# A transformer decoder layer with packed 4-bit weights: float16 weights from dequantization, and sixteen feed-forward chains run four at a time beside attention

## The chip, the cores and the metric

The kernel runs on one core of one Trainium2 chip. The metric is the time of one launch on the device, in microseconds. The engines are TensorE (PE; its weight loads appear as PEld), VectorE (DVE), ScalarE (ACT), GpSimd (POOL) and SyncE (SP), which here issues DMAs. Each engine works through its own queue in order, and waits for the others through semaphores.

## The reference, cut to what matters

Eight sequences (blocks b = 0 to 7) of 128 tokens with 512 features pass through causal self-attention, one cross attention against a context, and a gated feed-forward whose weights are packed 4-bit integers with group scales and zeros (GPTQ). The reference, shortened:

```
x = x + attn(layernorm(x), w_q, w_k, w_v, w_o)       # 32 heads of 128, 8 key/value heads
q = layernorm(x)
x = x + softmax(ctx @ q.T, axis=1) @ ctx             # key and value are both the context
def dequant_gptq(qweight, scales, zeros, groupsize): # groups of 128 rows
    zp = (z + 1.0) * s
    return q * s[g] - zp[g]
x2 = layernorm(x)                                    # 1024 x 512
gate, up = x2 @ Wg, x2 @ Wu                          # 512 -> 1376
x = x + ((gate * sigmoid(gate) * up) @ Wd).astype(float16)   # 1376 -> 512
```

The softmax of the cross attention divides by sqrt(128 context rows). Layernorm has no weights.

## The kernel before, in words

**Precision.** Most matmuls run on float16 pairs. A float32 value is split into a high part (`ah`, `qh`, `hi`) and a low part, the difference (`al`, `ql`, `lo`), and `mm3` (lines 159 to 165) adds three products. `split` (116) makes the high part on ACT and the low part on DVE or POOL. `convert` (349) scales a raw tile and splits it: by default with a POOL multiplication, an ACT copy and a POOL subtraction, and with `direct=True` with one scaled ACT copy (351) and one DVE multiply-subtract (352).

**Attention.** The work goes in 64 steps, one per key/value head group g (0 to 7) and block b. The last sixteen steps are (6, 0..3), (7, 0..3), (6, 4..7), (7, 4..7). A step takes the scores and softmax of a later block (`att_s`, 539), the projections of a later unit (`proj_q` and others), the output projection of the block before (`att_o`, 605, which adds to the residual `xr` on DVE at line 614) and the probabilities times values (`att_v`, 591). Probabilities `pb` are transposed to `pt` by a DMA on SP (588). PSUM has eight banks in four tags of two (186): "j" for projections, "s" for scores, "a", and "o" for outputs.

**Quantized weights.** In steps 8 to 42, 35 chunks are unpacked by `dequant` (738): a shift and mask, and then `q - 1 - z` written as int8 into `n8` (761). Scales aren't applied there: a feed-forward chain is a sum over groups, and between two groups the sum in PSUM is multiplied by the ratio of their scales. Before TensorE can use them, the int8 values are cast to float16: gate tiles on ACT (`nf_load`, 1024), up tiles on DVE (1026) and down tiles on ACT (`down_w`, 1162), each 128x512. From the fourth on, gate and up tiles go into buffers of the query weights (tags `wqh`, `wql`), and so wait until the projections have read these. These casts are called in steps 52 to 62.

**Cross attention.** The context is loaded from step 43 on (`c_load`, 911) and split by `c_prep` (915): POOL multiplies (919), ACT copies, POOL subtracts. A block whose attention has ended at step `done` gets `xA` (LayerNorm `norm_T` and a DMA transpose to `qT`, 907) one step later, `xB` (scores, softmax) two steps later, and `xC` (product, addition to `xr`) with `h3_load` (LayerNorm, transpose to `h3`, 1030) three steps later. Work due after step 63 goes into the event list below.

**Feed-forward.** Tokens are taken in two halves of 512. A half has 22 gate and up chains of four rounds (`gate_up`, 1130) and four down chains of eleven (`down`, 1164). A round (`Chain.emit`, 1107) is two matmuls (1114, 1115) into a bank, and then a rescaling of that bank, in turns on ACT (1123) and DVE (1125). A gate chain ends with Silu on ACT (1140); an up chain ends with a DVE product (1145), a high part (1151) and a low part (1152). Silu and the exponential need different tables on ACT, so a change between them issues a table load.

**What sets the order.** `events` holds the rounds with a slot number each (1203 to 1223). Four slots go with each of the last four steps (60 to 63), between the parts of attention; what is left follows after the last step. Chains 0 to 6 start two slots apart, and so run two at a time in the "j" banks (`EARLY = 7`); later ones start a slot apart and take "j", "s" and "o" in turn. Down chains start at slot `D0` = 29, the second half at `G1` = 40, its down chains at `D1` = 62. The order that is written is given to a scheduler, which places each engine's instructions by priority with its own model of time. `in_order` fixes the order on PE until step 59 and on POOL until the end of attention.

**Memory.** Pools are stacked from two sides. `xa` (right) holds context and cross-attention tiles; `fw` and `fp` (left, from step 52) hold float16 weights and products; high and low products `it` lie in query buffers (`qp`).

Of the kernel before, what the change touches and what calls it, by code (L numbers as in the profile page):

```python
# [8 lines left out]
F32 = mybir.dt.float32  # L9
# [1 line left out]
F16 = mybir.dt.float16  # L11
BF16 = mybir.dt.bfloat16
I32 = mybir.dt.int32
I8 = mybir.dt.int8
AF = mybir.ActivationFunctionType
ALU = mybir.AluOpType
PSUM = bass.MemoryType.PSUM
# [31 lines left out]
XPSCALE = 2.0**15  # L49
ROOT = 2.0**-104  # L50

NF0 = 3


@with_exitstack
def tile_decoder(
# [21 lines left out]
    def pool(name, bufs=1, **kw):  # L78
        return tc.alloc_tile_pool(name=name, bufs=bufs, **kw)
# [450 lines left out]
    def run(gen):  # L530
        for _ in gen:
            pass
# [72 lines left out]
    def att_o(g, b):  # L605
# [11 lines left out]


    sF = {}
    n8 = {  # L620
        "g": nqp.tile([P, KT, INTER], I8, name="n8g"),
        "u": nqp.tile([P, KT, INTER], I8, name="n8u"),
        "d": nqp.tile([P, NFT, H], I8, name="n8d"),
    }
    quant = {
        "g": (gq, gz, gs, KT, INTER),
# [111 lines left out]
    def dequant(m, g, c0, c1, after):  # L738
        qsrc = quant[m][0]
        n = c1 - c0  # L740
        rows = min(16, qsrc.shape[0] - g * 16)
        p = rows * 8
        qr = deqp.tile([P, H], I32, name="qr", tag="qr", bufs=2)
        nc.sync.dma_start(
            qr[:p, :n],
            qsrc[g * 16 : g * 16 + rows, c0:c1]
            .rearrange("r n -> r () n")
            .to_broadcast([rows, 8, n]),
        )
        zi = deqp.tile([P, H], I32, name="zi", tag="zi", bufs=2)  # L750
        row = zrow[m] + g
        nc.sync.dma_start(
            zi[:p, :n],
            zt["d"][row : row + 1, c0:c1].to_broadcast([p, n]),
        )
        qi = deqp.tile([P, H], I32, name="qi", tag="qi", bufs=1)
        ins = nc.vector.tensor_scalar(
            qi[:p, :n], qr[:p, :n], sh[:p], 15, ALU.logical_shift_right, ALU.bitwise_and
        )
        issue_after(ins, after)  # L760
        nc.vector.scalar_tensor_tensor(
            n8[m][:p, g, c0:c1], qi[:p, :n], -1.0, zi[:p, :n], ALU.add, ALU.subtract
        )

    chunks = []
# [143 lines left out]
            issue_after(ins, pace["dma"])  # L909

    def c_load(b):
        raw_t["c", b] = c = xa.tile([P, H], F32, name="c", tag="c", bufs=3)
        nc.sync.dma_start(c, cx[b])

    def c_prep(b):
        scales("c", b)
        ctx_scale(b)
        c = raw_t.pop(("c", b))
        ins = nc.gpsimd.tensor_tensor(
            c, c, scx[:, b : b + 1].to_broadcast([P, H]), ALU.mult  # L920
        )
        issue_after(ins, pace["mul"])
        cp = xa.tile([P, 2, H], F16, name="cp", tag="cp", bufs=B)
        split(cp[:, 0, :], cp[:, 1, :], c, nc.gpsimd)
        fl["c", b] = cp

    def norm_T(b, dst):
# [75 lines left out]
    for b in range(B):  # L1003
        at_x(XC + b, lambda b=b: c_load(b))
        at_x(XC + b + 1, lambda b=b: sumsq("c", b, 0, 0))
        at_x(XC + b + 3, lambda b=b: c_prep(b))
        done = steps.index((NG - 1, b))
        tail_x.setdefault((done + 1, 0), []).append(lambda b=b: xA(b))
        tail_x.setdefault((done + 2, 1), []).append(lambda b=b: xB(b))
        tail_x.setdefault((done + 3, 0), []).append(lambda b=b: (xC(b), h3_load(b)))  # L1010

    nf = {}

    def nf_load(m, t):
        w = min(P, INTER - t * P)
        if t < NF0:
            nf[m, t] = fw.tile([P, KT, P], F16, name="nf", tag="nf", bufs=2 * NF0)
        else:
            nf[m, t] = wqp.tile(
                [P, KT, P], F16, name="nf", tag={"g": "wqh", "u": "wql"}[m]  # L1020
            )
        src = n8[m][:, :, t * P : t * P + w]
        if m == "g":
            nc.scalar.copy(nf[m, t][:, :, :w], src)
        else:
            nc.vector.tensor_copy(nf[m, t][:, :, :w], src)

    h3 = {}

# [58 lines left out]

    FFN_MEM = len(steps) - 3 * HB
    FFN0 = len(steps) - HB
    PER_STEP = 4
    EARLY = 7
    ring = ["j", "s", "o"]
    count = [0, 0]

    class Chain:
# [8 lines left out]
        def emit(self, r):  # L1107
            if r == 0:
                count[0] += 1
                tag = "j" if count[0] <= EARLY else ring[count[0] % 3]  # L1110
                self.ps = bank(tag, [P, TH], "ps_c")
            ps = self.ps[: self.w]
            lh, rh, rl = self.parts(r)
            nc.tensor.matmul(ps, lh, rh, start=r == 0, stop=False, skip_group_check=r > 0)  # L1114
            nc.tensor.matmul(ps, lh, rl, start=False, stop=True, skip_group_check=r > 0)  # L1115
            if r == self.rounds - 1:
                self.finish(ps)
                return
            sc = self.ratios()[: self.w, r : r + 1]
            count[1] += 1  # L1120
            act = count[1] % 2 if self.act is None or r < 8 else self.act
            if act:
                nc.scalar.activation(ps, ps, AF.Copy, scale=sc)  # L1123
            else:
                nc.vector.tensor_scalar(ps, ps, sc, None, ALU.mult)  # L1125
# [4 lines left out]
    def gate_up(half, t, m):  # L1130
        w = min(P, INTER - t * P)

        def parts(g):
            return nf[m, t][:, g, :w], h3[half][:, 0, g, :], h3[half][:, 1, g, :]

        def finish(ps):
            sc = sF[m][:w, t, :]
            if m == "g":
                sg = fp.tile([P, TH], F32, name="sg", tag="sg")
                nc.scalar.activation(sg[:w], ps, AF.Silu, scale=sc)  # L1140
                sg_t[half, t] = sg
# [4 lines left out]
            if t < NFT - 1:  # L1146
                it = qp.tile([P, 2, TH], F16, name="it", tag="q" + "hl"[t % 2])
            else:
                it = fw.tile([P, 2, TH], F16, name="it", tag="it", bufs=1)
            eng = nc.vector if half and t >= NFT - 2 else nc.gpsimd  # L1150
            nc.vector.tensor_copy(it[:w, 0, :], pr[:w])  # L1151
            eng.tensor_tensor(it[:w, 1, :], pr[:w], it[:w, 0, :], ALU.subtract)  # L1152
            it_t[half, t] = it

        return Chain(KT, w, lambda: rT[m][:, t, :], parts, finish)

    nd_t = {}

    def down_w(g):
        w = min(P, INTER - g * P)  # L1160
        nd_t[g] = fw.tile([P, H], F16, name="nfd", tag="nfd", bufs=NFT)
        nc.scalar.copy(nd_t[g][:w], n8["d"][:w, g, :])

    def down(half, ct):
        cs = slice(ct * P, (ct + 1) * P)

        def parts(g):
            w = min(P, INTER - g * P)
            it = it_t[half, g]
            return nd_t[g][:w, cs], it[:w, 0, :], it[:w, 1, :]  # L1170

        def finish(ps):
            o = late[0].tile([P, TH], F32, name="oT", tag="oT", bufs=4)
# [21 lines left out]

    late = []

    def free_xa():
        xa.release()
        late.append(pool("late", side="right", reuse_waits="tile"))  # L1200


    NC = 2 * NFT
    events = []
    D0 = NC + EARLY
    G1 = D0 + NFT
    D1 = G1 + NC
    for half, (gs_, ds_) in enumerate([(0, D0), (G1, D1)]):
        for c in range(NC):
            ch = gate_up(half, c // 2, "gu"[c % 2])  # L1210
            st = gs_ + (c if half else c + min(c, EARLY))
            for r in range(KT):
                events.append((st + r, 1, c, lambda ch=ch, r=r: ch.emit(r)))
        for ct in range(KT):
            ch = down(half, ct)
            for r in range(NFT):
                st = ct * (0.5 if half else 1)
                events.append((ds_ + st + r, 1, NC + ct, lambda ch=ch, r=r: ch.emit(r)))
    for i, k in [i for i in tail_x if i[0] >= len(steps)]:
        slot = PER_STEP * (i - FFN0) + 1 + 2 * k  # L1220
        events.append((slot, 0, 1, lambda fs=tail_x.pop((i, k)): [f() for f in fs]))
    events.append((PER_STEP * (len(steps) + 5 - FFN0), 0, 1, free_xa))
    events.sort(key=lambda e: e[:3])

    def traced_after(n, engine, earlier):
# [16 lines left out]
    def tail_step(i):  # L1242
# [14 lines left out]
        for f in tail_x.pop((i, 0), ()):  # L1257
            f()
        run(parts)
        slots(3)  # L1260
        att_v(g, b)
        slots(4)
# [15 lines left out]
    for i in range(len(steps)):  # L1278
        known = len(nc.cur_bb.bb.instructions)
        if i == XC:  # L1280
            deqp.release()
            xa = pool("xa", 2, side="right", reuse_waits="tile")
        if i == FFN_MEM:
            rawp.release()
            fw = pool("fw", reuse_waits="tile")
            fp = pool("fp", 2, reuse_waits="tile")
        if i == FFN0:
            xt.update(s="a", o="a")
        pace["dma"] = pt_dma[steps[i + 1]] if i >= TAIL and steps[i + 1 :] and steps[i + 1] in pt_dma else None
# [17 lines left out]
            inter_scale()  # L1307
        for f in x_steps.pop(i, ()):
            f()
        for t in range(NFT):  # L1310
            if i == (FFN_MEM + 1 + t if t < NF0 else XATT - 4 + t):
                nf_load("g", t)
                nf_load("u", t)
        for g in range(NFT):
            if i == FFN_MEM + g:
                down_w(g)
        if i < 5 * HB:
            traced_after(known, last_h.ins.engine, last_h)
        if i == TAIL - 1:
# [8 lines left out]
    for e in events:  # L1328
        e[3]()

    for pl in (late[0], wvp, wkp, wqp, hp, fp, fw, qp, kp, vp, work, wop, psum, dram, nqp):
        pl.release()
    for pl in (small, xres, const):
        pl.release()
# [50 lines left out]
```

## Time and profile before

| | us |
|---|---|
| median of 3 runs | 676.97 (676.77 to 679.08) |
| the profiled execution | 678.71 |
| its span, first to last instruction | 676.7 |
| 512-column matmul, duration; start to start | 0.38; 0.215 |
| int8 to float16 cast on ACT (L1024, L1162); on DVE (L1026), least to most | 0.61; 0.36 to 2.67 |
| context: POOL multiply (L919), ACT copy, POOL subtract | 1.05, 0.62, 1.16 |
| rescaling on DVE (L1125), on ACT (L1123) | 0.75, 0.66 |
| high part of a product on DVE (L1151), low part on POOL (L1152) | 0.50, 1.15 |
| output addition on DVE (L614) | 0.75 |
| first feed-forward matmul; last attention output; first matmul of the second half | 518.7; 551.7; 601.4 |

A row of a timeline has the start in us from the beginning of the span, the duration, the engine, the line of the kernel, the instruction, `output<-inputs` by the program's names, and shapes; "x4" is four in a row. In brackets stand the idle time before it and the instruction that ended that. A row of the waits has the total, the number, and the longest.

### The profile page before, as it was taken

The page shows a single profiled execution, that of the slowest core. Times are in us where ns is not written, and L with a number is a line of the kernel's source. Part 1 is how long each engine was busy: PE and PEld are TensorE (multiplying, and loading weights), DVE is VectorE, ACT ScalarE, POOL GpSimd, SP SyncE. Part 2 cuts the span into 40 slices and gives each one's busy share as a digit, 9 for nine tenths or more (in the row PEclk, how much of TensorE's full clock was granted, in tenths as well). Part 3 has the DMA queues.
Part 4 walks back from the last instruction along what each step waited for, and adds up shares of the span by engine and source line. Part 5 has one row for each costly group of instructions (what it writes and reads, how often), then busy time and mean ns, then how long its engine had stood idle before and what let it go on. Part 6 is the DMA issues. An engine that isn't in the chain of part 4 may idle for free.

```text
span 676.7 us, 12449 instructions
## 1 busy us (share of the span) xinstructions
PE 639.2 (94%) x3978; PEld 341.6 (50%) x3978; DVE 480.2 (71%) x1504; ACT 453.2 (67%) x1261; POOL 400.6 (59%) x583
## 2 busy tenths in 40 slices
PE   8798999999999999999999999989989988999995
PEld 4365555455555555555555564544545443444442
DVE  6756587765757777676768464676777767988996
ACT  4587486655657574666667666796666667978674
POOL 5658287844747795555588497876775426521310
PEclk9988999999999999999999999999999999999998
DMA  9266344665453756455554525224433232202002
GB/s 309 49 154 176 97 62 117 163 126 148 112 155 87 188 128 157 104 159 127 160 142 109 134 37 136 54 57 87 84 74 56 55 59 48 47 16 62 1 1 62
DMA packets 117757, 69.34 MB, mean 102 GB/s; under 512 B 84174, under 2 KB 100577, under 8 KB 117692
## 3 DMA queue, kind: packets, MB, share of 16 engines
q1 hardware_dynamic: 117692, 68.55, 42.7%
q8 instruction: 31, 0.51, 0.3%
q14 instruction: 34, 0.28, 0.1%
HBM read 42.12 MB, written 2.20 MB: 65 GB/s over the span
## 4 chain that ended last, share of the span: by engine, by line
PE 54%; POOL 14%; DVE 9%; ACT 9%; issue 7%; DMA 6%; SPq 0%; POOLq 0%; DVEq 0%; ACTq 0%
PE ps_o L165 5%; PE ps_c L1114 5%; PE ps_o L163 5%; PE ps_o L164 5%; PE ps_c L1115 5%; PE ps_q L163 5%; PE ps_q L164 5%; PE ps_q L165 4%; DMA pt<-pb 3%; POOL pb L120 3%; POOL s L574 2%; DVE ps_c L1125 2%; POOL wol L120 2%; POOL rawo L357 1%; POOL wql L120 1%
## 5 line engine op out<-in xcount | busy, mean ns | idle before, releaser
L517 ACT ACTIVATE s<-s,negm 128x64 f32<-128x64 f32 (+1 forms) x256 | 93.2, 366 | 35.3 <-DVE negm L560 35.1
L165 PE MATMUL ps_o<-woh,al 128*128 128x512 f16 x256 | 97.3, 380 | 3.4 <-DVE al L120 3.2
L163 PE MATMUL ps_o<-woh,ah 128*128 128x512 f16 x256 | 97.3, 380 | 2.1 <-ACT ah L117 1.9
L163 PE MATMUL ps_q<-hT,wqh 128*128 128x512 f16 x256 | 97.4, 380 | 1.9 <-DVE ql L120 1.0
L165 PE MATMUL ps_q<-hT,wql 128*128 128x512 f16 x256 | 97.3, 380 | 0.0
L164 PE MATMUL ps_o<-wol,ah 128*128 128x512 f16 x256 | 97.3, 380 | 0.0
L164 PE MATMUL ps_q<-hT,wqh 128*128 128x512 f16 x256 | 97.3, 380 | 0.0
L614 DVE SCALAR_TENSOR_TENSOR xr<-ps_o,unsc,xr 128x512 f32<-128x512 f32 x64 | 47.8, 747 | 45.9 <-PE ps_o L165 42.4
L120 POOL TENSOR_TENSOR pb<-s,pb 128x256 f16<-128x256 f32 (+1 forms) x128 | 73.0, 585 | 10.3 <-ACT pb L117 8.6
L560 DVE CUSTOM_DVE_ANT_0 s<-ps_sc,mask,soft 128x64 f32<-128x64 f32 (+1 forms) x256 | 67.2, 310 | 7.3 <-PE ps_sc L165 6.6
L1114 PE MATMUL ps_c<-h,nf 128*128 128x512 f16 (+1 forms) x176 | 66.6, 379 | 3.9 <-ACT sg L1140 1.6
L1115 PE MATMUL ps_c<-h,nf 128*128 128x512 f16 (+1 forms) x176 | 66.6, 379 | 0.0
L574 POOL TENSOR_TENSOR s<-s,rec 128x128 f32<-128x128 f32 (+1 forms) x128 | 62.7, 510 | 4.5
L117 ACT CAST pb<-s 128x128 f16<-128x128 f32 (+1 forms) x128 | 43.2, 350 | 32.3 <-POOL s L574 31.1
L527 POOL TENSOR_SCALAR rec<-rec 128x4 f32<-128x4 f32 x64 | 14.7, 230 | 82.7 <-DVE rec L525 80.5
L120 DVE TENSOR_TENSOR ql<-ps_q,qh 128x512 f16<-128x512 f32 x64 | 43.9, 686 | 25.5 <-ACT qh L117 25.1
L1152 POOL TENSOR_TENSOR it<-pr,it 128x512 f16<-128x512 f32 (+1 forms) x20 | 23.1, 1154 | 63.9 <-DVE it L1151 53.3
L357 POOL TENSOR_TENSOR rawo<-rawo,sco 128x512 f32<-128x512 f32 x30 | 31.1, 1038 | 29.3 <-DVE sco L313 29.3
L120 DVE TENSOR_TENSOR al<-ps_at,ah 128x512 f16<-128x512 f32 x64 | 43.8, 684 | 6.5 <-ACT ah L117 6.3
L517 ACT ACTIVATION_READ_ACCUMULATOR s<-s,negm 128x1 f32 x256 | 48.1, 188 | 0.0
L117 ACT CAST ah<-ps_at 128x512 f16<-128x512 f32 x64 | 37.2, 581 | 14.8 <-PE ps_n L291 7.1
L1123 ACT ACTIVATE ps_c<-ps_c,rTu 128x512 f32<-128x512 f32 (+1 forms) x57 | 36.7, 661 | 12.9 <-PE ps_c L1115 12.3
(219 smaller groups left out, 1733.8 us busy)
## 6 DMA issues: line engine op xcount, KB each, us to landing
rawq<-in_L_attn_w_q_dram SPq DMA_DIRECT2D x8, 1024.0 KB, 6.5
rawo<-in_L_attn_w_o_dram SPq DMA_DIRECT2D x8, 1024.0 KB, 5.4
zi<-zd SPq DMA_DIRECT2D x26, 256.0 KB, 3.7
vd<-v SPq DMA_DIRECT2D x64, 64.0 KB, 2.4
qr<-_L_ffn_down_qweight_dram SPq DMA_DIRECT2D x10, 256.0 KB, 3.3
xr<-in_x_dram SPq DMA_DIRECT2D x8, 256.0 KB, 5.2
rawk<-in_L_attn_w_k_dram SPq DMA_DIRECT2D x8, 256.0 KB, 3.3
rawv<-in_L_attn_w_v_dram SPq DMA_DIRECT2D x4, 512.0 KB, 7.7
```

What stands on the lines that cost most here:

```text
L117: a = nc.scalar.copy(hi, src)
L120: b = (lo_eng or nc.vector).tensor_tensor(lo, src, hi, ALU.subtract)
L163: nc.tensor.matmul(ps, lh, rh, start=start and i == 0, stop=False)
L164: nc.tensor.matmul(ps, lh, rl, start=False, stop=False)
L165: nc.tensor.matmul(ps, ll, rh, start=False, stop=stop and i == n - 1)
L357: a = nc.gpsimd.tensor_tensor(raw, raw, wide.to_broadcast(list(raw.shape)), ALU.mult)
L517: exp = nc.scalar.activation(v, v, AF.Exp, bias=negm[:, j : j + 1], scale=-1.0, accum_out=sums[:, j : j + 1],)
L560: nc.vector.tensor_tensor_reduce(view, flat(ps, cols[j]), masks[j // 2], soft_t[g][:, j % 2 : j % 2 + 1], BIG, ALU.add, ALU.min, negm,)
L574: mul = nc.gpsimd.tensor_tensor(v, v, rec[:, 2 * k : 2 * k + 2].unsqueeze(2).to_broadcast([P, 2, (k + 1) * HQ]), ALU.mult,)
L614: return nc.vector.scalar_tensor_tensor(xr[b], ps, unsc_t[g], xr[b], ALU.mult, ALU.add)
L1114: nc.tensor.matmul(ps, lh, rh, start=r == 0, stop=False, skip_group_check=r > 0)
L1115: nc.tensor.matmul(ps, lh, rl, start=False, stop=True, skip_group_check=r > 0)
```

## The change

1. `dequant` writes float16 (`nf`) in place of int8 (`n8`); `nf_load`, `down_w` and the pool `fw` are gone, and chains read `nf` directly.
2. `c_prep` uses the direct form of `convert`: one scaled ACT copy, one DVE multiply-subtract.
3. `EARLY` is 16. These sixteen chains start one slot apart from slot 2 on, four at a time, in the banks of "j", "o", "j", "s" in turn. The six gate and up chains after them in the first half, and all of the second half, have their rounds 1.25 slots apart. `D0` is 24, so `G1` is 35 and `D1` 57.
4. Products `it` take query-weight buffers for the first eight and last four up chains, and query buffers between. In the second half the high part of the first nine goes to POOL.
5. `xC` and `h3_load` of blocks 0 to 2 come after the projections of their step.
6. The context has a pool of its own (`xc`, right), freed at slot 34 in place of 36; `xa` is opened on the left at step 52.

The diff, cut to its core:

```diff
-    n8 = {
-        "g": nqp.tile([P, KT, INTER], I8, name="n8g"),
...
+    nf = {
+        "g": nqp.tile([P, KT, INTER], F16, name="nfg"),
...
-            n8[m][:p, g, c0:c1], qi[:p, :n], -1.0, zi[:p, :n], ALU.add, ALU.subtract
+            nf[m][:p, g, c0:c1], qi[:p, :n], -1.0, zi[:p, :n], ALU.add, ALU.subtract
...
-        ins = nc.gpsimd.tensor_tensor(
-            c, c, scx[:, b : b + 1].to_broadcast([P, H]), ALU.mult
-        )
-        issue_after(ins, pace["mul"])
-        cp = xa.tile([P, 2, H], F16, name="cp", tag="cp", bufs=B)
-        split(cp[:, 0, :], cp[:, 1, :], c, nc.gpsimd)
+        cp = xc.tile([P, 2, H], F16, name="cp", tag="cp", bufs=B)
+        hi, lo = convert(cp[:, 0, :], cp[:, 1, :], c, scx[:, b : b + 1], True)
+        issue_after(hi, pace["exp"])
...
-        tail_x.setdefault((done + 3, 0), []).append(lambda b=b: (xC(b), h3_load(b)))
+        tail_x.setdefault((done + 3, 2 if b < HB - 1 else 0), []).append(lambda b=b: (xC(b), h3_load(b)))
...
-    EARLY = 7
+    EARLY = 16
...
-                tag = "j" if count[0] <= EARLY else ring[count[0] % 3]
+                tag = "sjoj"[count[0] % 4] if count[0] <= EARLY else ring[count[0] % 3]
...
-            return nf[m, t][:, g, :w], h3[half][:, 0, g, :], h3[half][:, 1, g, :]
+            return nf[m][:, g, t * P : t * P + w], h3[half][:, 0, g, :], h3[half][:, 1, g, :]
...
-            eng = nc.vector if half and t >= NFT - 2 else nc.gpsimd
-            nc.vector.tensor_copy(it[:w, 0, :], pr[:w])
-            eng.tensor_tensor(it[:w, 1, :], pr[:w], it[:w, 0, :], ALU.subtract)
+            hi_eng = nc.gpsimd if half and t < NFT - 2 else nc.vector
+            lo_eng = nc.vector if half and t >= NFT - 2 else nc.gpsimd
+            hi_eng.tensor_copy(it[0][:w], pr[:w])
+            lo_eng.tensor_tensor(it[1][:w], pr[:w], it[0][:w], ALU.subtract)
...
-    D0 = NC + EARLY
+    D0 = NC + 2
...
-            st = gs_ + (c if half else c + min(c, EARLY))
+            st = gs_ + c
             for r in range(KT):
-                events.append((st + r, 1, c, lambda ch=ch, r=r: ch.emit(r)))
+                events.append((st + (r if c < EARLY and not half else r * 1.25), 1, c, lambda ch=ch, r=r: ch.emit(r)))
...
-        for t in range(NFT):
-            if i == (FFN_MEM + 1 + t if t < NF0 else XATT - 4 + t):
-                nf_load("g", t)
-                nf_load("u", t)
-        for g in range(NFT):
-            if i == FFN_MEM + g:
-                down_w(g)
```

More of the change, by code (lines that the diff above doesn't have):

```diff
@@ L13 @@
 I32 = mybir.dt.int32
-I8 = mybir.dt.int8
 AF = mybir.ActivationFunctionType
@@ L50 @@
 ROOT = 2.0**-104
-NF0 = 3
 @with_exitstack
@@ L619, in tile_decoder @@
     sF = {}
-    n8 = {
-        "g": nqp.tile([P, KT, INTER], I8, name="n8g"),
-        "u": nqp.tile([P, KT, INTER], I8, name="n8u"),
-        "d": nqp.tile([P, NFT, H], I8, name="n8d"),
+    nf = {
+        "g": nqp.tile([P, KT, INTER], F16, name="nfg"),
+        "u": nqp.tile([P, KT, INTER], F16, name="nfu"),
+        "d": nqp.tile([P, NFT, H], F16, name="nfd"),
     }
@@ L911, in c_load @@
     def c_load(b):
-        raw_t["c", b] = c = xa.tile([P, H], F32, name="c", tag="c", bufs=3)
+        raw_t["c", b] = c = xc.tile([P, H], F32, name="c", tag="c", bufs=3)
         nc.sync.dma_start(c, cx[b])
@@ L1009, in tile_decoder @@
         tail_x.setdefault((done + 2, 1), []).append(lambda b=b: xB(b))
-        tail_x.setdefault((done + 3, 0), []).append(lambda b=b: (xC(b), h3_load(b)))
[L1012 to L1026, printed above, removed]
+        tail_x.setdefault((done + 3, 2 if b < HB - 1 else 0), []).append(lambda b=b: (xC(b), h3_load(b)))
     h3 = {}
@@ L1145, in finish @@
             nc.vector.scalar_tensor_tensor(pr[:w], ps, sc, sg[:w], ALU.mult, ALU.mult)
-            if t < NFT - 1:
-                it = qp.tile([P, 2, TH], F16, name="it", tag="q" + "hl"[t % 2])
-            else:
-                it = fw.tile([P, 2, TH], F16, name="it", tag="it", bufs=1)
-            eng = nc.vector if half and t >= NFT - 2 else nc.gpsimd
-            nc.vector.tensor_copy(it[:w, 0, :], pr[:w])
-            eng.tensor_tensor(it[:w, 1, :], pr[:w], it[:w, 0, :], ALU.subtract)
+            u = half * NFT + t
+            if 8 <= u < 8 + 10:
+                it = qp.tile([P, 2, TH], F16, name="it", tag="q" + "hl"[u % 2])
+                it = it[:, 0, :], it[:, 1, :]
+            else:
+                it = [
+                    wqp.tile([P, TH], F16, name="it" + p, tag="wq" + p) for p in "hl"
+                ]
+            hi_eng = nc.gpsimd if half and t < NFT - 2 else nc.vector
+            lo_eng = nc.vector if half and t >= NFT - 2 else nc.gpsimd
+            hi_eng.tensor_copy(it[0][:w], pr[:w])
+            lo_eng.tensor_tensor(it[1][:w], pr[:w], it[0][:w], ALU.subtract)
             it_t[half, t] = it
         return Chain(KT, w, lambda: rT[m][:, t, :], parts, finish)
[L1157 to L1162, printed above, removed]
     def down(half, ct):
@@ L1169, in parts @@
             it = it_t[half, g]
-            return nd_t[g][:w, cs], it[:w, 0, :], it[:w, 1, :]
+            return nf["d"][:w, g, cs], it[0][:w], it[1][:w]
         def finish(ps):
@@ L1196, in tile_decoder, with free_xc @@
     late = []
-    def free_xa():
-        xa.release()
+    def free_xc():
+        xc.release()
         late.append(pool("late", side="right", reuse_waits="tile"))
@@ L1204, in tile_decoder @@
     events = []
-    D0 = NC + EARLY
+    D0 = NC + 2
     G1 = D0 + NFT
     D1 = G1 + NC
-    for half, (gs_, ds_) in enumerate([(0, D0), (G1, D1)]):
+    for half, (gs_, ds_) in enumerate([(2, D0), (G1, D1)]):
         for c in range(NC):
             ch = gate_up(half, c // 2, "gu"[c % 2])
-            st = gs_ + (c if half else c + min(c, EARLY))
+            st = gs_ + c
             for r in range(KT):
-                events.append((st + r, 1, c, lambda ch=ch, r=r: ch.emit(r)))
+                events.append((st + (r if c < EARLY and not half else r * 1.25), 1, c, lambda ch=ch, r=r: ch.emit(r)))
         for ct in range(KT):
@@ L1219, in tile_decoder @@
     for i, k in [i for i in tail_x if i[0] >= len(steps)]:
-        slot = PER_STEP * (i - FFN0) + 1 + 2 * k
+        slot = PER_STEP * (i - FFN0) + (1, 3, 2)[k]
         events.append((slot, 0, 1, lambda fs=tail_x.pop((i, k)): [f() for f in fs]))
-    events.append((PER_STEP * (len(steps) + 5 - FFN0), 0, 1, free_xa))
+    events.append((min(PER_STEP * (len(steps) + 5 - FFN0), D0 + NFT - 1), 0, 1, free_xc))
     events.sort(key=lambda e: e[:3])
@@ L1259, in tail_step @@
         run(parts)
+        for f in tail_x.pop((i, 2), ()):
+            f()
         slots(3)
@@ L1281, in tile_decoder @@
             deqp.release()
-            xa = pool("xa", 2, side="right", reuse_waits="tile")
+            xc = pool("xc", 2, side="right", reuse_waits="tile")
         if i == FFN_MEM:
             rawp.release()
-            fw = pool("fw", reuse_waits="tile")
             fp = pool("fp", 2, reuse_waits="tile")
+            xa = pool("xa", 2, reuse_waits="tile")
         if i == FFN0:
@@ L1329, in tile_decoder @@
         e[3]()
-    for pl in (late[0], wvp, wkp, wqp, hp, fp, fw, qp, kp, vp, work, wop, psum, dram, nqp):
+    for pl in (late[0], wvp, wkp, wqp, hp, xa, fp, qp, kp, vp, work, wop, psum, dram, nqp):
         pl.release()
```

## The prediction

> **What bounds the kernel now.** I read the page first, then the windows, then PE's waits, then the timelines around each wait.
>
> ```profile
> span 676.7 us, 12449 instructions
> ...
> PE 639.2 (94%) x3978; PEld 341.6 (50%) x3978; DVE 480.2 (71%) x1504; ACT 453.2 (67%) x1261; POOL 400.6 (59%) x583
> ```
>
> Windows, in us: length, then PE, PEld, DVE, ACT and POOL busy, granted clock, DMA share, GB/s.
>
> ```profile
> 440.00:460.00 20.00, 17.18 (x105) 9.39 (x104) 14.29 (x51) 19.71 (x58) 14.27 (x21) 0.91 0.27 66
> ...
> 480.00:500.00 20.00, 18.45 (x127) 9.56 (x126) 15.37 (x57) 12.26 (x38) 13.38 (x21) 1.00 0.47 87
> ...
> 560.00:580.00 20.00, 16.49 (x80) 6.98 (x79) 16.45 (x36) 16.99 (x28) 11.88 (x14) 1.00 0.30 55
> ...
> 620.00:640.00 20.00, 19.91 (x93) 9.02 (x92) 18.80 (x34) 14.28 (x24) 6.87 (x6) 1.00 0.05 14
> ```
>
> PE sets the end, so only PE gaps can be won. There are few before 420. Three stretches matter: 440 to 460, where ACT is full and the clock falls to 0.91; 464 to 516; and 540 to 601. From 601 to 660 PE is full again, though DVE is at 90%. A 512-column matmul lasts 0.38 us but the next starts 0.215 later, so I measure gaps from start to start.
>
> The first stretch, in the timelines of ACT, DVE and PE:
>
> ```profile
> 449.76 2.16 ACT L1162 CAST nfd<-n8d 128x512 f16<-128x512 int8 x4
> 451.82 0.61 ACT L1024 CAST nf<-n8g 128x512 f16<-128x512 int8 x1
> 452.34 0.57 ACT L117 CAST qh<-ps_q 128x512 f16<-128x512 f32 x1
> ```
>
> ```profile
> 452.95 0.69 DVE L120 TENSOR_TENSOR ql<-ps_q,qh 128x512 f16<-128x512 f32 x1 [1.10 <-ACT qh L117]
> ```
>
> ```profile
> 453.70 0.28 PE L163 MATMUL ps_v<-wvh,hT 128*128 128x256 f16 x1 [1.76 <-DVE softx L323]
> ```
>
> ps_v waits for a bank that qh and ql free. Their input was complete at 445, but qh stood behind eleven int8 casts on ACT. The wait is booked on a tiny DVE instruction; ql, ended at 453.64, is the real one. A gap of 1.2 us, on the transposed probabilities (pt), has just gone before, and PE runs at half clock from 454.0 to 457.4 (256-column matmuls 0.21 apart instead of 0.11).
>
> **The change part by part.**
>
> *(a) Casts removed, 440 to 458.* Twenty-two ACT casts at 0.61 (12.9 us with the short ones) and eleven on DVE (9.1) go; sixteen and five of them lie in 440:460. The gaps are 1.22 and 1.92, and the slow clock adds 1.9: 5.0. Nothing else on ACT fills the place, since ACT without the 9.3 us is at half load. The wait at 451.22 is also POOL's: pb's subtraction started at 446.93, after a `cp` subtraction (445.82, 1.16) that the change moves off POOL. Bounds 4 to 5; I take **-4.7**.
>
> *(b) Casts removed, 464 to 516.* Six pairs are left here, one per step, each just ahead of qh and ql.
>
> ```profile
> PE ps_o L165 <- DVE al L120: 3.2, 4, 1.1
> ```
>
> ```profile
> 494.30 0.62 ACT L1024 CAST nf<-n8g 128x512 f16<-128x512 int8 x1 [1.49 <-PE ps_q L164]
> ```
>
> ```profile
> 495.44 0.69 DVE L120 TENSOR_TENSOR ql<-ps_q,qh 128x512 f16<-128x512 f32 x1 [0.49 <-ACT qh L117]
> ```
>
> Each is followed within 4 us by a PE gap on ql or al: 0.55, 0.51, 0.59, 1.27, 1.18, 1.06, together 5.2. A pair delays qh, ql and al by about 0.6, so a gap shrinks by the smaller of 0.6 and itself: 0.55+0.51+0.59+0.6+0.6+0.5. Bounds 2 and 4.5; I take **-3.3**. What is late next is al itself.
>
> *(c) Context split.* Eight times a POOL multiplication (1.05), ACT copy (0.62) and POOL subtraction (1.16) become an ACT scaled copy (0.72) and a DVE multiply-subtract. POOL sheds 17.7 us, ACT takes 0.8 more, and DVE's eight like it in the prologue (L352) took 7.6 in all, 0.73 to 1.13 each. Here a rule speaks against the change. The Trainium skill, "SBUF — State Buffer", "Who interferes with whom": a DVE instruction with two SBUF inputs shares a read port with GpSimd, and whoever comes second waits for the whole instruction. This one has two. By the rule each may wait out a POOL instruction, 0.75+1.16=1.9, so 15 us; by the row 7.6. The trace shows the lock on a cast (L1026: 0.36 to 2.67 us), yet the L352 row was taken with POOL 60% busy too, so I use 7.6, less than the 9.1 of casts that leave DVE. The DVE instruction waits for its ACT half, with ql, al and the softmax rows queued behind and PE behind those. Bounds: -1 (POOL, freed, no longer delays pb), and 4 (half a microsecond each, as in b); DVE idles 20.4 of the 60 us from 420 to 480, so I stay near the first: **+1.0**. The SP queue gains, as context loads waited there for `cp` (20.2 us).
>
> *(d) Chains four at a time, from step 60.* A half has 22 gate and up chains of 4 rounds and 4 down chains of 11, 132 rounds of two matmuls (0.433 us). The event list places 31 rounds before slot 16, the end of the last attention step (the trace has 31 there too); the new list places 50. So 19 rounds, 8.2 us of PE, move ahead of the last attention output at 551.9. PE's work is unchanged; the worth is the gaps from 540 to 601, about 10 us start to start, where few chains are open and each round waits for the rescaling before it (0.75 on DVE, 0.66 on ACT). Against it stands the serial end: last output, LayerNorm, cross attention, LayerNorm, transpose, first chain of the second half.
>
> ```profile
> 551.67 0.38 PE L165 MATMUL ps_o<-woh,al 128*128 128x512 f16 x1
> ...
> 601.37 0.38 PE L1114 MATMUL ps_c<-h,nf 128*128 128x512 f16 x1 [0.23 <-DMA h<-hb]
> ```
>
> It takes 49.5 us now, and PE arrives 0.2 early: just in time. Unqueued it is 21.5: two LayerNorms of 7.3 (1.15 DVE, 1.35 POOL, 0.61 ACT, 1.16 POOL, 3.05 DMA), scores 0.7, softmax with a table load 4, product and adds 2.2. Afterwards PE has 76 rounds, three scores and three products under it: 32.9+4.0=36.9. Gaps of 4.4 in this stretch now (95 rounds give 45.1). I take 2.4 afterwards, the path needing 39.3, and 1 us won before 551.9. Bounds: -9 (nearly all gaps) and +7 (ACT, below); **-3.0**.
>
> Load in steps 60 to 63, each: PE 12.5 rounds 5.4 + output 2.6 + 1.0 = 9.0. DVE: rows 1.6, al 0.7, xr 0.75, norm 1.3, 4.7 rescalings 3.5, 1.6 products and copies 1.9 = 9.7. ACT: exponentials 2.0, pb/ah/hb 1.9, rescalings 3.1, Silu 1.1, table loads.
>
> ```profile
> 557.24 1.28 ACT L517 ACT_TABLE_LOAD   x1
> 558.53 0.40 ACT L517 ACTIVATE xs<-xs,negm 128x128 f32<-128x128 f32 x1
> ```
>
> Silu and exp alternate: nine loads now from 530 on, and up to two more if Silu falls between the last attention softmaxes. The Trainium skill, "ScalarE: Activation LUTs", "What ACT_TABLE_LOAD costs", gives 1.28 for the load and 1.38 for a drain. Here the instruction before ended at 557.21 and the next starts at 558.53, so 1.3 is all. Two extra cost ACT 2.6 by the row, 5.3 by the rule. With two loads a step ACT needs 10.7: it is near the bound, 1.7 above PE.
>
> The chains take one of two score and output banks at a time; a score bank is read out in 1.6 us and ps_o in 0.75, so I cost the lost double buffering at nothing while steps last 9 us; if DVE lags, up to 0.75 a step, 3 us, inside the bounds of (d).
>
> *(e) Second half.* Nine high parts (0.50 each, 4.5 us) move from DVE to POOL. No POOL cast is in the trace; POOL's h<-xr (0.77) and subtraction (1.16) bound it at 0.5 to 1.2; I take 0.8. With the subtraction that is 2 us of POOL per pair of chains (3.5 us of PE), on an empty engine. PE idles 0.3 from 600 to 660: **-0.3**, from 0 to -0.7.
>
> *(f) Costed at nothing.* Float16 instead of int8 from dequantization: 35 writes of 0.69 median on DVE, from 118 to 379 where PE is 98.6% busy; that cover hides it, and without it a tenth of a microsecond each way would be 3.5. The cross-attention products of blocks 0 to 2 move behind their step's projection, with all they issue: three matmuls (0.65), DVE's add, the next LayerNorm on DVE, POOL and ACT, and its transpose on SP. They pass 2.6 us of projection; the first chain (518.7) waits for block 3, which keeps its place; if the transpose then falls behind a pt, up to its 1.2 us. The ups' other buffers are read last by projections before 514; the later start and earlier release reorder but add nothing. The last 10 us (down, transpose, store) stay.
>
> **Sum.** -4.7-3.3+1.0-3.0-0.3 = -10.3. The profiled execution took 678.71 around its span of 676.7, 1.7 above the median of 676.97; it would become 668.4, and the median **666.7**.
>
> **Rivals.**
> *Full fill:* the path ends in under 36.9 us, nothing waits: -4.7-4.5-9-0.3 = 658.5. For: it needs only 21.5. Against: 49.5 today with the same engines beside it.
> *Exchange of waits:* the path shrinks only to 45. The last output ends at 551.9-7.0+8.2-1=552, the second half starts at 597, 4.4 earlier: 672.3. For: just-in-time at 601.37.
> *Slower: ACT bounds steps 60 to 63.* 1.7 a step, 6.8, delays the last output to 559.9; with the path still 49.5 the second half starts at 609.4: +8.0-0.3 = 684.7. It decides once that delay and the path, counted from 553.1, together pass 52. Against: in 520:540 ACT was busy 13.5 of 20 with PE full.
>
> **Chances.** Forecast (661 to 671) 0.52; full fill 0.15; exchange 0.23, half of it under 673.6; slower 0.10. A measurement tells 0.5% (3.4 us) from no change. Faster 0.52+0.15+0.12=0.79, same 0.11, slower 0.10. The range 656 to 677 leaves out the slower case and the outer ends of two others.
>
> **What would show it.** (a): clock 1.00 in the stretch after 440, no ACT cast, ps_v without 1.8. (b): PE's waits on al under 1.5. (c): eight DVE subtractions of 0.75 to 1.1, none ahead of a PE gap. (d): about 50 rounds before the last ps_o, and the wait of the first second-half chain on the transpose: 0 to 3 us if I am right, over 5 in the exchange. (e): DVE under 85% there. I am wrong if ACT fills in steps 60 to 63 or the path stays near 50 us.

## The result and the profile after

The median is 672.25 us (671.60 to 672.98) against 677.73 (676.77 to 679.08) for the kernel before beside it: a ratio of 0.9918, 95% interval 0.9895 to 0.9941, or 5.5 us. A second set of runs of the changed kernel gave 671.88 and 0.9920 (0.9901 to 0.9938). The forecast was 666.7, with 656 to 677 as its range: the direction is right, and the gain about half. The experiments will show that even this half came together from terms that were wrong one by one.

The page of the profiled execution (671.60 us; busy time, share and instructions of each engine):

```profile
span 669.8 us, 12405 instructions
...
PE 633.9 (95%) x3978; PEld 340.5 (51%) x3978; DVE 476.0 (71%) x1492; ACT 443.1 (66%) x1239; POOL 389.8 (58%) x576
```

The windows, with the columns of before:

```profile
440.00:460.00 20.00, 19.68 (x132) 11.29 (x130) 15.66 (x61) 12.25 (x37) 7.46 (x16) 1.00 0.39 84
...
480.00:500.00 20.00, 19.42 (x150) 10.72 (x147) 15.92 (x67) 12.56 (x44) 11.76 (x19) 1.00 0.45 77
...
560.00:580.00 20.00, 17.84 (x95) 8.28 (x94) 18.67 (x45) 13.48 (x23) 10.22 (x12) 1.00 0.23 41
...
620.00:640.00 20.00, 20.00 (x94) 9.35 (x93) 16.41 (x24) 15.19 (x24) 10.33 (x12) 1.00 0.01 2
```

ACT falls from 19.7 to 12.3 busy in 440 to 460, and PE rises from 17.2 to 19.7 at full clock. In 560 to 580 PE still idles over 2 us. The pair `qh`, `ql` of the first stretch, on ACT and then on DVE, now has no cast in front of it, and the wait of 1.76 on `ps_v` is gone:

```profile
450.11 0.56 ACT L115 CAST qh<-ps_q 128x512 f16<-128x512 f32 x1
```

```profile
450.90 0.69 DVE L118 TENSOR_TENSOR ql<-ps_q,qh 128x512 f16<-128x512 f32 x1
```

PE's wait on `al`, the low half of the attention output, from 464 to 516 (total, number, longest):

```profile
PE ps_o L163 <- DVE al L118: 1.2, 3, 0.6
```

It was 3.2. Then the serial end of attention, on PE: the last output and the first matmul of the second half.

```profile
560.38 0.38 PE L163 MATMUL ps_o<-woh,al 128*128 128x512 f16 x1
...
594.66 0.38 PE L1094 MATMUL ps_c<-h,nfg 128*128 128x512 f16 x1 [0.20 <-DMA h<-hb]
```

The last output comes 8.7 us later than before, with 56 rounds of chains ahead of it in place of 31; the path behind it, from start to start, shrinks from 49.7 us to 34.3. Five moments of the two PE timelines:

| us | before | after | difference |
|---|---|---|---|
| one group of `ps_o` matmuls near 420 | 421.5 | 420.0 | -1.6 |
| last `ps_q` | 512.1 | 504.3 | -7.8 |
| first chain | 518.7 | 514.4 | -4.4 |
| first matmul of the second half | 601.4 | 594.7 | -6.7 |
| last transpose, `ps_f` | 670.2 | 662.6 | -7.7 |

The first 1.6 aren't the change's: in a second profile of the changed kernel this group starts at 421.7, as before. From there to the last `ps_q`, 6.2 are won (forecast for a, b and c: 7.0), and from there to the second half 1.1 are lost (forecast for d: 3.0 won). That looks like three terms right and one wrong. It isn't so: 3.4 of the 6.2 are gone by the first chain. The last `ps_q` is a poor mark, because the cross-attention products now come behind the projections, with their waits; the experiments measure the terms better.

### The profile page after: what moved, and what is told of

The parts are those of the page before. It is cut to its first block, busy times and chain, and to the rows that moved or that the text cites. A ratio compares the mean times of both kernels' runs of the same rounds, so it can differ in the third digit from the quotient of the medians.

```text
span 669.8 us, 12405 instructions
## 1 busy us (share of the span) xinstructions
PE 633.9 (95%) x3978; PEld 340.5 (51%) x3978; DVE 476.0 (71%) x1492; ACT 443.1 (66%) x1239; POOL 389.8 (58%) x576
## 4 chain that ended last, share of the span: by engine, by line
PE 47%; POOL 18%; issue 9%; DVE 9%; ACT 8%; DMA 8%; SPq 0%; POOLq 0%; DVEq 0%; ACTq 0%
PE ps_c L1094 5%; PE ps_c L1095 5%; PE ps_o L163 5%; PE ps_o L161 4%; PE ps_o L162 4%; PE ps_q L161 4%; PE ps_q L163 4%; PE ps_q L162 4%; POOL pb L118 4%; POOL s L572 3%; DMA pt<-pb 3%; ACT ps_c L1103 2%; POOL wql L118 2%; POOL wol L118 2%; DVE ps_c L1105 2%
## 5 line engine op out<-in xcount | busy, mean ns | idle before, releaser
L1103 ACT ACTIVATE ps_c<-ps_c,rTu 128x512 f32<-128x512 f32 (+1 forms) x64 | 40.9, 661 | 14.9 <-PE ps_c L1095 14.9
L1105 DVE TENSOR_SCALAR ps_c<-ps_c,rTg 128x512 f32<-128x512 f32 (+1 forms) x63 | 45.6, 750 | 5.3 <-PE ps_c L1095 4.9
L115 ACT CAST qh<-ps_q 128x512 f16<-128x512 f32 x64 | 36.8, 575 | 16.1 <-PE ps_q L163 16.0
L161 PE MATMUL ps_sc<-k,qh 128*128 128x128 f16 (+1 forms) x256 | 41.5, 207 | 2.2 <-ACT qh L115 2.0
```

The lines of the kernel that those rows point to most:

```text
L115: a = nc.scalar.copy(hi, src)
L161: nc.tensor.matmul(ps, lh, rh, start=start and i == 0, stop=False)
```

## The experiments

All times are medians in us; a ratio is to the kernel before, run beside each of the three sets (677.06, 677.98 and 677.54 us), with its 95% interval. Sets ran on different chips, so ratios compare them better than medians. In the diffs, `...` marks lines left out.

### One part at a time: casts and context

**Casts alone.** In the changed kernel the old chain schedule, the context split on POOL, the high parts on DVE and the old place of `xC` are put back:

```diff
-    EARLY = 16
+    EARLY = 7
...
-        hi, lo = convert(cp[:, 0, :], cp[:, 1, :], c, scx[:, b : b + 1], True)
-        issue_after(hi, pace["exp"])
+        ins = nc.gpsimd.tensor_tensor(c, c, scx[:, b : b + 1].to_broadcast([P, H]), ALU.mult)
...
+        split(cp[:, 0, :], cp[:, 1, :], c, nc.gpsimd)
...
-            hi_eng = nc.gpsimd if half and t < NFT - 2 else nc.vector
+            hi_eng = nc.vector
...
-        tail_x.setdefault((done + 3, 2 if b < HB - 1 else 0), []).append(lambda b=b: (xC(b), h3_load(b)))
+        tail_x.setdefault((done + 3, 0), []).append(lambda b=b: (xC(b), h3_load(b)))
```

> Only the casts are removed here (float16 weights from dequantization, and the memory that this needs); the chain schedule, the context split on POOL, the high parts on DVE and the place of the product of the cross attention are those of the kernel before. The prediction's terms (a) and (b) say -8.0, so 669.7 against 677.7 (669 to 671); the last ps_q before the feed-forward comes at about 504 and the wait on al under 1.5 us. Theory (the chains gave nothing, the casts gave about all): 669 to 672, no slower than the changed kernel's 672.25. Rival (the chains gave the forecast 3, and casts and context less than forecast): 674 to 676.

Measured: 676.22 (ratio 0.9985, 0.9969 to 1.0000). Neither theory holds: removing 22 casts from ACT and 11 from DVE gives 1.0 us where the prediction had 8.0.

**Context alone.** The kernel before with only the direct form of the context split:

```diff
-        ins = nc.gpsimd.tensor_tensor(c, c, scx[:, b : b + 1].to_broadcast([P, H]), ALU.mult)
...
-        split(cp[:, 0, :], cp[:, 1, :], c, nc.gpsimd)
+        hi, lo = convert(cp[:, 0, :], cp[:, 1, :], c, scx[:, b : b + 1], True)
...
```

> The kernel before with the context split alone made direct (one ACT scaled copy and one DVE multiply-subtract); the int8 casts and the old chains stay. Removing the casts alone gave -0.9 us, undoing the direct form in the changed kernel cost +4.7. If the direct form is worth its 4.7 by itself (POOL's late subtraction held back the context's buffers, their loads, and ACT behind the loads): 671.5 to 674. If ACT's and POOL's load hide one another, so that both have to go before PE gains anything (the casts then stand in the place of ACT's wait on the load): 675.5 to 678. The prediction's +1.0 by itself: 678.

Measured: 677.45 (0.9986, 0.9978 to 0.9995), again 1 us.

**Both.** The kernel of "casts alone", with this same edit:

> Casts removed and context split direct; chains, high parts of products and the place of the cross-attention product as before. If casts and context split make up the gain: 671.5 to 673.5, the same as the changed kernel. If the later parts (chains, high parts on POOL, moved product) carry 1 us or more of it: 673.5 to 675.

Measured: 673.36 (0.9932, 0.9919 to 0.9945). One and one make 2.0, but both together give 4.6. The reverse says the same:

**Context back on POOL, everything else changed:**

```diff
-        hi, lo = convert(cp[:, 0, :], cp[:, 1, :], c, scx[:, b : b + 1], True)
...
+        ins = nc.gpsimd.tensor_tensor(c, c, scx[:, b : b + 1].to_broadcast([P, H]), ALU.mult)
...
+        split(cp[:, 0, :], cp[:, 1, :], c, nc.gpsimd)
```

> The changed kernel with the context split on POOL put back (POOL multiplication, ACT copy, POOL subtraction). The prediction's term (c), +1.0 for the direct form, says 671.2 (bounds 668 to 673). Theory (the direct form takes POOL out of the way of pb and costs DVE nothing where it idles): 672.5 to 674, with gaps on pt or pb back in the stretch 440 to 480.

Measured: 676.94 (0.9991, 0.9979 to 1.0004): 4.7 above the changed kernel, and no better than before, with all its casts gone. Why, its ACT timeline shows:

```profile
453.61 0.63 ACT L259 ACTIVATE junk<-c 128x512 bf16<-128x512 f32 x1 [2.82 <-DMA c<-in_ctx_dram]
...
454.50 0.61 ACT L115 CAST cp<-c 128x512 f16<-128x512 f32 x1
455.01 0.59 ACT L115 CAST ah<-ps_at 128x512 f16<-128x512 f32 x1
```

PE in the same moment:

```profile
455.65 0.39 PE L161 MATMUL ps_o<-woh,ah 128*128 128x512 f16 x1 [1.48 <-ACT ah L115]
```

ACT stands still for 2.8 us in front of the sum of squares of a context tile whose load hasn't come, with `v`, `cp` and `ah` queued behind. The waits from 425 to 480, ACT's and then the DMA queue's own, say where the load was:

```profile
ACT junk L259 <- DMA c<-in_ctx_dram: 7.1, 3, 2.8
```

```profile
SPq L911 <- POOL cp L118: 10.2, 3, 7.2
```

The load waits on SP for one of three raw context buffers; POOL's subtraction, the last reader, frees it late. The kernel before had this wait too, but ACT waited there for only 1.7: the int8 casts filled the time. Its rows:

```profile
ACT junk L261 <- DMA c<-in_ctx_dram: 1.7, 1, 1.7
```

```profile
SPq L913 <- POOL cp L120: 16.5, 3, 7.2
```

With the casts alone removed ACT's wait is 7.0 as well. So the casts were in part a filler, and when they go the wait for the load stands there.

**The same with five buffers.**

```diff
-        raw_t["c", b] = c = xc.tile([P, H], F32, name="c", tag="c", bufs=3)
+        raw_t["c", b] = c = xc.tile([P, H], F32, name="c", tag="c", bufs=5)
```

> The changed kernel with the context split on POOL put back as in the run that took 676.9, but with five buffers for the raw context in place of three, so that two more loads go out without waiting for POOL's last subtraction. If the loss of 4.7 comes by the buffer, the late load and ACT's statistics pass that waits for it ahead of the next ah, then ACT's wait on the load (7.1 us from 425 to 480) falls to under 3, the gaps on ah and al at 455 to 457 (1.65 and 1.01) shrink or move later, and the time is 672.5 to 675. If POOL's own load is the cause (pb behind the subtractions): the time stays at 676 to 678.

Measured: 673.67 (0.9930, 0.9918 to 0.9942). The same two views:

```profile
ACT junk L259 <- DMA c<-in_ctx_dram: 0.9, 2, 0.7
```

```profile
SPq L911 <- POOL cp L118: 2.6, 1, 2.6
```

POOL still does all its work, and 3.3 of the 4.7 us are back (by the ratios 4.1 of 4.9): it was the buffer, not mainly POOL's load. The gaps of 1.65 and 1.01 us at 455 to 457 are down to one of 0.72. The rest, 1.4 or by the ratios 0.8, lies within the intervals; it may be POOL's or nothing.

Why the direct form didn't help by itself is in the ACT timeline of the kernel with only that:

```profile
441.40 2.17 ACT L1159 CAST nfd<-n8d 128x512 f16<-128x512 int8 x4
443.48 0.72 ACT L351 ACTIVATE cp<-c,scx 128x512 f16<-128x512 f32 x1
444.10 1.64 ACT L1159 CAST nfd<-n8d 128x512 f16<-128x512 int8 x3
445.65 0.57 ACT L117 CAST ah<-ps_at 128x512 f16<-128x512 f32 x1
```

Its PE:

```profile
446.28 0.39 PE L163 MATMUL ps_o<-woh,ah 128*128 128x512 f16 x1 [2.19 <-ACT ah L117]
```

Here the loads come in time, and `ah` stands behind seven casts instead. Two obstacles lay over one another on one in-order queue; each alone suffices to make `ah` late.

The traces show a second exchange, on PE. In 464 to 516 the wait on `al` falls to 0.8 us when casts and context are gone, from 3.2, but now PE waits for the probabilities of the cross attention (`xph` and `xpl`, high and low part), 4.4 in place of 0.2; with the casts alone gone, 3.5:

```profile
PE ps_xo L163 <- DVE xpl L966: 3.6, 4, 1.3
...
PE ps_xo L161 <- ACT xph L965: 0.8, 2, 0.6
```

With the product moved behind the projections (change 5) these waits are 0.8. What that is worth in time comes below.

### High parts on POOL

```diff
-            hi_eng = nc.gpsimd if half and t < NFT - 2 else nc.vector
+            hi_eng = nc.vector
```

> The changed kernel with all high parts of the products on DVE again. The prediction's term (e), -0.3 (0 to -0.7), says 672.5 (672.2 to 673). The trace shows the second half 1.0 us shorter after than before; if that is the high parts' doing: 673.2.

Measured: 671.82 (0.9905, 0.9890 to 0.9921), as fast as the changed kernel: the move is worth nothing that can be measured. POOL's cast took 0.61 us (guessed at 0.8), and PE was busy 59.7 of the 60 us from 600 to 660 even before.

### The chains

**The old schedule alone put back**, run twice:

```diff
-    EARLY = 16
+    EARLY = 7
...
-    D0 = NC + 2
+    D0 = NC + EARLY
...
-            st = gs_ + c
+            st = gs_ + (c if half else c + min(c, EARLY))
...
```

> The changed kernel with the chain schedule of before alone put back (seven early chains two slots apart in the banks of j, first at slot 0, down chains at slot 29). Theory (four at a time gave nothing: the gaps that it closes late it opens at the start of step 60): 671 to 673, the same as 672.25 within 0.2%; last ps_o at about 544, 31 rounds before it. Rival (the chains gave the forecast 3 and something else took it): 674.5 to 676.

> The changed kernel with the old chain schedule once more, to size term (d) on one chip. If four chains at a time gave the forecast 3: 675.2. If they gave nothing: 672.6, within 1 of the changed kernel.

Beside the second, the changed kernel again:

> The changed kernel once more, beside the others on one chip: 672.25 (671.6 to 673).

Measured: 672.61 (0.9935, 0.9919 to 0.9950) and 672.50 (0.9931, 0.9905 to 0.9956), against 672.25 and 671.88. Four chains at a time are worth 0.4 to 0.6 by medians, 0.8 to 1.2 by ratios, and the intervals overlap; the forecast was 3.0. Since casts and context gave 673.36, what the moved product and the high parts add is no more than 0.9 by medians, and nothing by ratios. From 420 on, the old chain schedule with the product moved has its last `ps_q` 4.6 us earlier than with the product in its old place, and its first chain only 0.5 earlier: that is the poor mark.

**First chain at slot 0**, and down chains at 22 in place of 24:

```diff
-    D0 = NC + 2
+    D0 = NC
-    for half, (gs_, ds_) in enumerate([(2, D0), (G1, D1)]):
+    for half, (gs_, ds_) in enumerate([(0, D0), (G1, D1)]):
```

> The changed kernel with the first chain at slot 0 in place of 2, and the down chains two slots earlier (22, not 24), so that about 58 rounds would come before the last ps_o. If the gaps at 504 to 520 (0.7, 0.6, 0.5, 1.2) are there because no chain is open yet, they shrink and the time is 670 to 671.5. If the exchange is within the banks or in the rescaling, nothing is won: 672 to 673.5. If the first chains wait for the transpose of block 3 at 514 whatever their slot, the same as 672.25.

Measured: 676.80 (0.9995, 0.9983 to 1.0006), 4.5 slower; none of the three. PE, at the first down chain and at the second half:

```profile
574.38 0.38 PE L1094 MATMUL ps_c<-ith,nfd 128*128 128x512 f16 x1 [2.07 <-ACT sg L1120]
...
602.28 0.38 PE L1094 MATMUL ps_c<-h,nfg 128*128 128x512 f16 x1 [0.47 <-DMA h<-hb]
```

The first row waits for a Silu still under way; 106 rounds in place of 89 come before the last cross-attention product, which falls at 591.1 (581.0 in the changed kernel), and the second half starts 7.6 us later. So an earlier start, with the down chains moved along, doesn't help. Which of the two edits does the harm wasn't separated.

**What do the chains wait for?** PE's waits in the changed kernel, 514 to 602, the largest:

```profile
PE ps_c L1094 <- ACT sg L1120: 1.9, 3, 0.8
PE ps_c L1094 <- ACT ps_c L1103: 1.3, 2, 0.9
PE ps_at L595 <- DMA pt<-pb: 1.0, 1, 1.0
PE ps_c L1094 <- DVE ps_c L1105: 0.7, 2, 0.5
```

All of them make 6.7, against 6.3 before (where the transpose `qT` had 2.2 and `sg` 1.6). Waits of chains on a bank that attention still reads (`xr`, `rec`) are 1.0 after and 0.8 before, so sharing banks isn't it. At the head are Silu and the rescalings behind it on ACT, and the table loads between exp and Silu are nine as before:

```profile
551.22 1.28 ACT L515 ACT_TABLE_LOAD   x1
552.51 0.40 ACT L515 ACTIVATE xs<-xs,negm 128x128 f32<-128x128 f32 x1
```

The longest wait of a chain, with what stands before it on ACT:

```profile
537.56 1.28 ACT L515 ACT_TABLE_LOAD   x1
...
539.26 1.22 ACT L1103 ACTIVATE ps_c<-ps_c,rTu 128x512 f32<-128x512 f32 x2
```

```profile
539.95 0.38 PE L1094 MATMUL ps_c<-h,nfu 128*128 128x512 f16 x1 [0.95 <-ACT ps_c L1103]
```

So the loads were taken away, by leaving the Silu out and copying in its place. Such a kernel doesn't compute the layer, but a copy takes as long as a Silu (0.69 us):

```diff
-                nc.scalar.activation(sg[:w], ps, AF.Silu, scale=sc)
+                nc.scalar.activation(sg[:w], ps, AF.Copy, scale=sc)
```

> The changed kernel with the Silu of the gate chains left out (a scaled copy in its place, the output is no longer the layer's): ACT loads no table between Silu and exp (nine loads of 1.28, 11.5 us of ACT, after). If PE's waits in the feed-forward beside attention, 6.7 us from 514 to 602, hang on these loads (a bank is held until the table is in, and rescalings stand behind it): the waits fall to 3 or less and the time to 667.5 to 669.5. If they hang on the serial path of attention and on the rescalings themselves: 671 to 672.5.

> The same without Silu, with the old chain schedule. If the table loads ate what four chains at a time should have given, the old schedule is now 2 to 3.5 us slower than the new one without Silu. If four at a time gives nothing even without the loads: within 1 us of it.

Measured: 667.00 (0.9842, 0.9821 to 0.9864) with the new schedule, 670.61 (0.9894, 0.9876 to 0.9911) with the old. The window 514 to 602 of the changed kernel, then of the same without Silu:

```profile
514.00:602.00 88.00, 80.68 (x415) 37.87 (x414) 69.97 (x151) 65.80 (x121) 39.47 (x50) 1.00 0.27 46
```

```profile
514.00:602.00 88.00, 85.01 (x442) 40.49 (x441) 75.58 (x176) 59.50 (x128) 41.18 (x55) 1.00 0.29 52
```

PE's waits fall from 6.7 to 2.6, its busy time rises by 4.3. With the old schedule the waits fall only from 7.1 to 5.0.

| us | old schedule | four at a time | difference |
|---|---|---|---|
| with Silu | 672.50 | 671.88 | 0.6 |
| Silu left out | 670.61 | 667.00 | 3.6 |

Nine loads take 11.5 us of an engine that is busy 66 of 88; by the medians they cost 1.9 us in the old schedule and 4.9 in the new. Without them four at a time gives 3.6, about what was forecast. The runs of the two schedules don't overlap then (665.62 to 667.85 and 669.43 to 670.86); with Silu they do. Where the cost lies, PE's gaps show. They are counted from start to start, less 0.215 us for every 512 columns, between the first chain and the first matmul of the second half:

| gaps of PE, us | up to the last attention output | behind it |
|---|---|---|
| before | 2.9 | 8.6 |
| changed | 6.6 | 4.8 |
| changed, Silu left out | 1.6 | 3.4 |
| changed, old schedule (second run) | 4.9 | 7.1 |
| the same, Silu left out | 3.7 | 6.5 |

Before and after, the sums are 11.6 and 11.4: what four chains at a time took away behind the last output came back ahead of it, and goes with the loads. A load holds up more than its own chain: the bank whose Silu waits stays full for 2.0 us (1.28 + 0.69) instead of 0.7, and the rescalings of the other open chains stand behind it on ACT. That more open chains make a load dearer fits these figures; since banks and slots changed with the number of chains, it isn't shown by itself.

## Why the prediction was half right

**(a) and (b), the casts: -8.0 forecast, -1.0 alone.** The failing sentence is "Nothing else on ACT fills the place, since ACT without the 9.3 us is at half load". Half load was right (12.3 of 20), but load wasn't the question. What filled the place was a wait: 7.0 us from 425 to 480 for context loads, hidden under the casts before. The row that tells it was in the text already, "context loads waited there for `cp` (20.2 us)", and was named as a gain of (c) without a figure. In (b), "What is late next is al itself" missed the cross attention: with the casts alone gone, PE waited 3.5 us there for `xph` and `xpl`, and 0.8 for `al`. (By its own rule the last of the six gaps of (b) should count 0.6, not 0.5; that is a tenth.)

**(c), the context: +1.0 forecast, -3.6 to -4.7 beside the removed casts, -0.9 without.** The sign was wrong. The bound of -1 counted POOL's delay of `pb` and not the buffer that POOL frees, the load behind the buffer, and ACT behind the load. The durations were sized nearly rightly: the eight subtractions took 8.4 us (7.6 forecast). Four took 0.75 us, the others 0.91, 1.17, 1.62 and 1.68, which the rule on the shared read port allows and the 1.13 of the earlier row didn't. None stands ahead of a PE gap: the three waits of PE from 410 to 470 are for `ah` from ACT (1.41, and 1.46 before; 0.33; 0.32).

Together a, b and c were forecast at -7.0 and gave -4.6. Errors of 7 and 5 us of opposite sign left one of 2.4. That the sum was so much better than its parts is luck. Where the 2.4 went isn't shown; the waits for `xph` and `xpl` are the candidate in the trace.

**(d), the chains: -3.0 forecast, -0.4 to -1.2.** The wait of the second half was 0.2, as hoped, and 56 rounds came before the last output (50 forecast). The path of 34.3 us (39.3) was near by errors that cancel. The reading of 95 rounds behind the last output was wrong: the trace of the kernel before has 86 there (172 matmuls), and gaps of 8.6, not 4.4. After the change there are 62 rounds (76 forecast) and two blocks' cross attention in place of three, 29.5 us of work for 36.9, and gaps of 4.8 for the 2.4 that it took. The step that failed is "1 us won before 551.9": ahead of the last output the gaps grew by 3.7 us, and ate the 3.8 won behind it. Table loads were priced as busy time of ACT, with two more as the risk. They stayed nine and took the gain as latency in front of open chains.

**(e) and (f): -0.3 and 0; both within what the runs can tell.** The high parts gave nothing, the moved product 0.9 at most, though it took 3.6 us of PE's waits in 464 to 516. PE was 99.1% busy from 118 to 379, not 98.6; the float16 writes there cost nothing that a mark shows, as the group near 420 starts at 421.5 before and at 420.0 and 421.7 in two profiles after. DVE fell from 91% to 88% in 600 to 660, not under 85%.

**The rivals.** The exchange of waits said 672.3, by chance to the decimal: it had the last output at 552 and a path of 45, where 560.4 and 34.3 came. That waits were exchanged was right, but the new ones stand ahead of the last output and not in the path behind it. The slower case fell: the last output did come at 560, as it said, but the path behind it had shrunk.

**The signs that were named** were nearly all met: clock 1.00, `al` at 1.2, the wait of the second half at 0.2. They couldn't tell what a part is worth from its having happened: the kernel with the context back on POOL also shows `al` at 1.4 and no cast, at 676.94.

**Open:** whether the 0.8 to 1.4 us that five buffers don't bring back are real; whether the moved product is worth up to 0.9, and why no more, given the waits that it removes; which edit of the early start harms; how much of a load's cost is due to the number of open chains. No kernel that computes the whole layer was clearly faster than the changed one.

## What to carry to other kernels

When two things stand in front of the same in-order engine, removing one shows the other: before a busy stretch is booked as a gain, look for the waits that lie under it, whose loads and buffers they are, and price the edits together. A table load is not just busy time: look at what stands behind it on the queue and at whose banks stay full. Here it undid an interleaving that was worth 3.6 us without it. Grouping the functions before interleaving is the next thing to try; no run here did.

## What the runs showed of the hardware

The granted clock isn't a fixed part of a program's time. The changed kernel with the old chains was profiled twice, with the same wait of 1.6 us on `xph` near 543 in both: one trace shows a granted clock of 0.91 in 546 to 556, with 512-column matmuls 0.43 us apart from 544.3 to 547.5; the other shows 1.00, with 0.215. The gaps of 1.5 and 1.0 us near 455 went without a slower clock with the casts alone removed, and with 0.90 and 0.93 around them with the context on POOL. In 27 runs of the kernel before, the mean clock went from 0.988 to 0.997. So the 1.9 us that the prediction gave the slow clock in (a) need not be there in every execution; the kernel before was profiled only once.

The two longest of the eight DVE subtractions of the context, 1.62 and 1.68 us, each began within 0.1 us after a POOL subtraction with two inputs in SBUF:

```profile
431.46 1.15 POOL L118 TENSOR_TENSOR wol<-rawo,woh 128x512 f16<-128x512 f32 x1
```

```profile
431.48 1.68 DVE L350 SCALAR_TENSOR_TENSOR cp<-c,scx,cp 128x512 f16<-128x512 f32 x1 [0.84 <-ACT cp L349]
```

The four of 0.75 us fell where POOL was idle. So the lock that the prediction quoted is seen here, at somewhat less than the 1.9 us that it worked out.
